# Cross-attention in split fp32: one PSUM bank for each unit of both products, first passes scaled in place, the bias and the residual waiting in the result tile

## The chip, the cores and the metric

The kernel runs on one NeuronCore of a Trainium2 chip. The metric is the device time of one execution in microseconds. A profile records one execution: its span runs from the first to the last instruction, and the device time is a little longer than the span. Five engines run side by side, each in the order of its own instruction list: PE (matrix products), DVE (vector), ACT (scalar), POOL and SP. SP and POOL mostly start DMA transfers; POOL also reduces across partitions. PE writes its sums into PSUM, a memory of eight banks of 128 x 512 fp32 values.

## What is computed

Eight batches, each with `x1` and `x2` of 512 channels by 1024 positions:

```python
q = jnp.einsum('bcn,dc->bnd', x1, Wq) + bq          # D = 64
k = jnp.einsum('bcn,dc->bdn', x2, Wk) + bk[:, None]
v = jnp.einsum('bcn,dc->bdn', x2, Wv) + bv[:, None] # 512 channels
attn = jax.nn.softmax(jnp.einsum('bnd,bdm->bnm', q, k), axis=2)
attn_out = jnp.einsum('bcm,bnm->bcn', v, attn)
return attn_out + x1
```

All of it is fp32. The two large products are "the value product" (v) and "the result product" (attn_out).

## The kernel before

**Splitting.** A plain fp32 product of 128 x 128 by 128 x 512 takes two records on PE, 0.43 us each on the chain that ended last (22 of them in 9.44 us); the type fp32r (fp32 rounded to fewer bits) takes one of 0.23 us (16 in 3.63 us). So an operand is split into a high part h, a low part l and a third part d = a mixture of the two scaled by T = 4096, and one exact product becomes three fp32r passes: h by h, l by l, d by d. h by h and l by l are summed in one PSUM bank ("X"), d by d in another ("Y"); the product is (T+1) times X joined with Y, up to a factor T.

**Units.** A batch has eight value units j (128 positions by 512 channels) and eight result units u (128 queries by 512 channels). A value unit takes 12 passes (`VX`: 8 into X, `VY`: 4 into Y); a result unit takes 24 (`R.u.m` for m = 0 to 7: one d pass into Y, then h and l into X). Before a value unit's `VY`, ACT writes the bias times T into the Y bank (`sy`). After it ACT copies Y to SBUF (`cy`), DVE joins X with it (`jn`), and the pair of units is split again: `vh` on ACT, `vl` and `vd` on DVE, 128 x 1024 values each. After a result unit ACT takes Y out, scaled by the reciprocal of the softmax sum (`oy`), DVE joins X with it (`o`), POOL adds x1 transposed by an accumulating DMA into the result tile (`oa`), and SP stores it (`st`). Units 6 and 7 of the first seven batches leave before the reciprocal is there, and ACT scales them later (`os`). The last batch's units 6 and 7 get x1 from a loaded tile on DVE (`lt`, `t`), and its unit 7 leaves in two parts (`o`, `p`).

**Scores and softmax.** `Q` and `K` are plain fp32 products (`qe`, `qd`, `qr`, `ql` and the same for k take them out, repeat and split them). `S.h.i` are the 16 blocks of scores of a batch, two passes each; `Sc` copies one to SBUF on ACT; `F` folds the maximum on DVE, `T` reduces it across partitions on POOL, `L` subtracts it on DVE, `E` takes the exponential on ACT, `H`, `l`, `d` split a unit of it. `es`, `a1` (an accumulating DMA from POOL), `a2`, `a3`, `tot` and `few` form the softmax sums of a quarter (two units), `rec` the reciprocal, `r2` two scaled copies of it.

**Batch one** (the first) has plain fp32 in three value units (`VF`, joined by `jf`) and in result units 0 and 1 (`RF`, taken out by `of`), since the split parts are not there yet.

**Order.** The order of all this is written out by hand as three strings of such words: FIRST for batch one, MIDDLE for the six that follow, LAST for the eighth. A word with "+" belongs to the next batch, with "-" to the one before. Each engine gets its own words in that order and the tile pools place the waits. PSUM: three X banks, three Y banks, two score banks ("sc"), each used in turn, so the fourth X unit waits until the first one's X bank has been read.

Of the kernel before, what the change touches and what calls it, by code (L numbers as in the profile page):

```python
# [35 lines left out]
vd.2 +Q +qe +ldx2.1 S.1.2 Sc.1.2 VY.6 cy.6 jn.6 S.1.3 Sc.1.3 S.1.4 Sc.1.4 S.1.5 Sc.1.5 T.1 L.3 S.1.6 Sc.1.6
VX.7 S.1.7 sy.7 VY.7 E.0 RF.0.0 RF.0.1 RF.0.2 RF.0.3 RF.0.4 RF.0.5 E.1 es.0 RF.1.0 a1.0 L.2 Sc.1.7 F.2 T.2
RF.1.1 E.3 H.3 l.3 a2.0 RF.1.2 RF.1.3 E.2 H.2 es.1 l.2 a1.1 a3.0 +qd +qr +ql RF.1.4 cy.7 jn.7 vh.3 +ldx2.0 +K
+ke RF.1.5 L.5 E.5 RF.0.6 L.4 E.4 H.4 RF.1.6 d.2 RF.0.7 RF.1.7 R.2.0 vl.3 tot.0 few.0 rec.0 r2.0 of.1 oa.1 F.3
of.0 d.3 es.2 R.2.1 R.2.2 R.2.3 R.2.4 R.2.5 R.3.0 R.3.1 R.3.2 R.3.3 R.3.4 a2.1 a3.1 +kc +kr +kl +S.0.0 +S.0.2  # L40
+Sc.0.0 H.5 l.4 R.3.5 st.1 +S.0.1 +Sc.0.1 +Sc.0.2 vd.3 R.2.6 R.3.6 T.3 L.6 L.7 E.7 +S.0.3 +Sc.0.3 R.2.7 R.3.7
d.4 R.4.0 R.4.1 a1.2 a2.2 +S.0.4 +S.0.5 tot.1 few.1 rec.1 oa.0 st.0 a3.2 l.5 d.5 E.6 H.6 l.6 d.6 tot.2 few.2
r2.1 oy.2 oy.3 o.2 o.3 oa.2 oa.3 st.2 st.3 H.7 l.7 rec.2 +Sc.0.4 +Sc.0.5 R.4.2 R.4.3 R.4.4 R.4.5 R.4.6 R.4.7
+S.0.6 +Sc.0.6 d.7 +S.0.7 +Sc.0.7 +F.0 es.3 a1.3 r2.2 oy.4 o.4 oa.4 st.4 +xh.0 +xl.0 +xd.0 +xh.1 +xl.1 R.5.0
R.5.1 R.5.2 R.5.3 R.5.4 R.5.5 R.5.6 R.5.7 oy.5 o.5 +T.0 +L.0 +L.1 +E.0 +E.1 +es.0 oa.5 st.5 a2.3 a3.3 +F.1
+xd.1 R.6.0 R.6.1 R.6.2 R.6.3 R.6.4 R.6.5 R.6.6 R.6.7 oy.6 o.6 +S.1.0 +xh.2 +xl.2 +xd.2 +sy.0 R.7.0 R.7.1
R.7.2 R.7.3 +xh.3 +xl.3 tot.3 few.3 rec.3 +sy.1 +Sc.1.0 +S.1.1 +Sc.1.1 R.7.4 R.7.5 R.7.6 R.7.7 oy.7 o.7
"""
MIDDLE = """
VY.0 cy.0 VX.0 +ldx1.0 a1.0 sy.2 jn.0 T.1 L.2 L.3 sy.3 VX.1 VY.1 cy.1 jn.1 H.1 l.1 H.0 l.0 d.0 vh.0 vl.0 vd.0  # L50
S.1.2 Sc.1.2 VY.2 cy.2 VX.2 jn.2 S.1.4 +ldx1.1 d.1 VY.3 cy.3 VX.3 jn.3 sy.4 E.2 S.1.3 Sc.1.3 Sc.1.4 sy.5 VX.4
-r2.3 -os.6 -oa.6 -st.6 S.1.5 Sc.1.5 xd.3 a2.0 a3.0 VY.5 cy.5 VX.5 vh.1 vl.1 vd.1 S.1.6 Sc.1.6 VY.4 cy.4 jn.4
# [24 lines left out]
r2.2 oy.4 oy.5 o.4 oa.4 st.4 l.7 o.5 oa.5 st.5 d.7 R.7.0 R.7.7 rec.3 r2.3 oy.6 oy.7 t.6 t.7 o.6 o.7 p.7 st.6
st.7 sq.7
# [4 lines left out]
def kernel(  # L83
# [31 lines left out]
    seed = const.tile([P, C], F32, name="bv_seed")  # L115
# [18 lines left out]
    class Batch:  # L134
        def __init__(self, b):
            self.b = b
            self.first = b == 0
            self.final = b == B - 1
            self.x1, self.x2, self.ps = {}, {}, {}
            self.half, self.fold, self.top, self.es, self.den, self.few, self.r = {}, {}, {}, {}, {}, {}, {}  # L140
            self.c, self.e, self.v, self.v4 = {}, {}, {}, {}
            self.X, self.Y, self.y, self.o = {}, {}, {}, {}
# [65 lines left out]
        def take_out(self, which):  # L210
            t = new([P, N], "es" if self.first else "v4", f"{'qk'[which]}_{self.b}")
            for h, r in ((0, lo), (1, hi)):
                nc.scalar.activation(
                    t[r, ts(h, H)], self.ps[which][r, :], AF.Identity, bias=bqk_sb[r, which : which + 1]
                )
            return t
# [43 lines left out]
        def S(self, h, i):  # L260
            self.ps[h, i] = ps = bank("Y" if self.first and i % 2 else "sc", f"ps_s_{self.b}_{h}_{i}")
# [42 lines left out]
        def d(self, u):  # L304
            e = self.e[u]
            e["d"] = new([P, MT, P], "kd", f"ed_{self.b}_{u}", FR)
            nc.vector.scalar_tensor_tensor(e["d"], f32(e["l"]), -T, f32(e["h"]), ALU.mult, ALU.add)  # L307
# [29 lines left out]
        def rec(self, Q):  # L337
            self.r[Q] = new([P, 2, 2], "r", f"r_{self.b}_{Q}")
            nc.vector.reciprocal(self.r[Q][:, 0, :], self.few[Q])

        def r2(self, Q):
            r = self.r[Q]
            nc.scalar.mul(r[:, 1, :], r[:, 0, :], 1.0 / T)
            nc.scalar.mul(r[:, 0, :], r[:, 0, :], 1.0 + 1.0 / T)
# [26 lines left out]

        def VF(self, j, c):
            if c == 0:
                self.X[j] = bank("X", f"ps_v_{self.b}_{j}")
            nc.tensor.matmul(  # L375
                self.X[j], self.chunk(j // 2)[:, c, ts(j % 2, P)], wraw[c // 2][:, c % 2, :],
# [3 lines left out]
        def pair(self, j):  # L380
            if j % 2 == 0:
                tag = ("kh" if j < 4 else "kl") if self.first else "v4"
                self.v4[j // 2] = new([P, 2, C], tag, f"v4_{self.b}_{j // 2}")
            return self.v4[j // 2][:, j % 2, :]

        def jf(self, j):
            nc.vector.scalar_tensor_tensor(self.pair(j), self.X[j], T, seed, ALU.mult, ALU.add)

        def sy(self, j):
# [196 lines left out]
```

## Time and profile before

| what | value |
|---|---|
| time, median of 3 runs | 660.4 us (660.15 to 660.41) |
| span of the profiled execution | 657.9 us |
| the profiled execution's own device time | not given apart from the runs; the median lies 2.5 us over the span |
| PE busy | 652.4 us (99%), 2797 products |
| DVE busy | 615.3 us (94%) |
| ACT busy | 451.0 us (69%) |
| POOL busy | 204.6 us (31%) |
| DMA | 90.21 MB, 137 GB/s over the span |

Busy times are sums over instructions of one engine. PE's records overlap: one lasts 0.39 us and the next starts 0.23 us after it. So the pace of PE is read from the chain that ended last, where each piece counts only the step.

### The profile page before, as it was taken

The numbers are of one execution on the slowest core, as the hardware profiler recorded it, in microseconds if no ns is written. First come the engines' busy times: TensorE is split into PE (matmuls) and PEld (weight loads), VectorE is DVE, ScalarE is ACT, GpSimd is POOL, SyncE is SP. The second block draws the span as 40 slices with busy tenths as digits, with TensorE's granted clock in tenths as the row PEclk, the third lists the DMA queues.
The fourth block names the chain that finished last, engine by engine and source line by source line (L and its number), as shares of the span: only waits on it lengthen the run. The fifth ranks groups of instructions, "written<-read, shape, count | busy, mean of one in ns | idle before, by whom it ended". The sixth has DMA issues, their size and how long they took to land.

```text
span 657.9 us, 8049 instructions
## 1 busy us (share of the span) xinstructions
PE 652.4 (99%) x2797; PEld 491.6 (75%) x2797; DVE 615.3 (94%) x689; ACT 451.0 (69%) x668; POOL 204.6 (31%) x162
## 2 busy tenths in 40 slices
PE   9999999999999999999999999999999999999997
PEld 3664888668886688866888668886688776887786
DVE  5789999999999999999999999999999999989994
ACT  5597748767587675875767767687675975759541
POOL 0024532423314343033520335221352214412451
PEclk9999999999999999999999999999999999999999
DMA  8544466564656556374563746737467274642374
GB/s 312 197 143 85 96 134 185 102 187 90 143 152 148 140 115 167 104 200 108 117 173 90 210 96 121 170 83 220 81 128 185 73 206 100 124 113 48 64 137 136
DMA packets 41464, 90.21 MB, mean 137 GB/s; under 512 B 13136, under 2 KB 13904, under 8 KB 37712
## 3 DMA queue, kind: packets, MB, share of 16 engines
q0 software_dynamic: 13536, 33.04, 30.1%
q1 hardware_dynamic: 27168, 56.14, 25.7%
q10 hardware_dynamic: 720, 0.53, 0.2%
q8 instruction: 22, 0.36, 0.2%
q14 instruction: 18, 0.15, 0.1%
HBM read 51.91 MB, written 16.78 MB: 104 GB/s over the span
## 4 chain that ended last, share of the span: by engine, by line
PE 94%; DVE 3%; ACT 2%; issue 0%; DVEq 0%; ACTq 0%
PE ps_oX L435 33%; PE ps_oY L435 17%; PE ps_vX L395 15%; PE ps_s L263 8%; PE ps_vY L395 8%; PE ps_k L206 4%; PE ps_q L206 4%; PE ps_o L460 2%; PE ps_v L375 2%; PE ps_warm L535 1%; DVE vd L427 1%; DVE vl L422 0%; DVE v L413 0%; ACT ps_vY L391 0%; DVE ed L307 0%; DVE e L291 0%
## 5 line engine op out<-in xcount | busy, mean ns | idle before, releaser
L435 PE MATMUL ps_oY<-vd,ed 128*128 128x512 f32 x496 | 193.8, 393 | 0.2 <-DVE ed L307 0.2
L435 PE MATMUL ps_oX<-vh,eh 128*128 128x512 f32 x496 | 193.0, 389 | 0.0
L435 PE MATMUL ps_oX<-vl,el 128*128 128x512 f32 x496 | 193.0, 389 | 0.0
L435 PEld LDWEIGHTS ps_oY<-vd,ed 128*128 128x128 f32 x496 | 93.1, 188 | 25.1 <-issue 5.3
L515 POOL DMA_DIRECT2D o<-in_x1T_dram x62 | 55.6, 917 | 172.2 <-ACT o L512 100.0
L435 PEld LDWEIGHTS ps_oX<-vl,el 128*128 128x128 f32 x496 | 93.0, 188 | 20.2
L435 PEld LDWEIGHTS ps_oX<-vh,eh 128*128 128x128 f32 x496 | 93.1, 188 | 19.5 <-DVE v L413 0.3
L294 ACT ACTIVATE e<-e 128x1024 f32<-128x1024 f32 x64 | 67.7, 1061 | 54.7 <-DVE e L291 53.6
L268 ACT COPY e<-ps_s 128x512 f32<-128x512 f32 x128 | 71.0, 591 | 32.7 <-PE ps_s L263 31.8
L330 POOL PARTITION_ALL_REDUCE den<-es x32 | 82.1, 2565 | 23.3 <-DVE es L320 20.2
L316 POOL DMA_DIRECT2D es<-e x32 | 28.6, 894 | 181.7 <-ACT es L313 172.3
L307 DVE SCALAR_TENSOR_TENSOR ed<-el,eh 128x1024 fp32r<-128x1024 f32 x62 | 81.9, 1321 | 2.1
L302 DVE TENSOR_TENSOR el<-e,eh 128x1024 fp32r<-128x1024 f32 x62 | 79.7, 1302 | 0.0
L291 DVE TENSOR_TENSOR e<-e,top 128x1024 f32<-128x1024 f32 x64 | 76.1, 1220 | 1.0 <-POOL top L283 1.0
L283 POOL PARTITION_ALL_REDUCE top<-max x32 | 46.8, 1463 | 65.3 <-DVE max L279 65.2
L395 PE MATMUL ps_vX<-wh,xh 128*128 128x512 f32 x244 | 66.1, 393 | 0.0
L395 PE MATMUL ps_vX<-wl,xl 128*128 128x512 f32 x244 | 65.2, 389 | 0.0
L395 PE MATMUL ps_vY<-wd,xd 128*128 128x512 f32 x244 | 64.7, 392 | 0.4 <-ACT ps_vY L391 0.4
L298 ACT ACTIVATE eh<-e 128x1024 fp32r<-128x1024 f32 x62 | 64.7, 1055 | 0.5
L410 ACT COPY vy<-ps_vY 128x512 f32<-128x512 f32 x61 | 36.0, 592 | 37.5 <-PE ps_vY L395 37.3
L395 PEld LDWEIGHTS ps_vX<-wh,xh 128*128 128x128 f32 x244 | 45.3, 188 | 14.3 <-DVE max L278 4.1
L395 PEld LDWEIGHTS ps_vY<-wd,xd 128*128 128x128 f32 x244 | 45.5, 188 | 11.8 <-issue 1.3
(59 smaller groups left out, 963.3 us busy)
## 6 DMA issues: line engine op xcount, KB each, us to landing
x<-in_x_dram SPq DMA_DIRECT2D x29, 1024.0 KB, 7.0
es<-e POOLq DMA_DIRECT2D x32, 512.0 KB, 4.9
out_dram<-o SPq DMA_DIRECT2D x63, 256.0 KB, 2.4
o<-in_x1T_dram POOLq DMA_DIRECT2D x62, 256.0 KB, 4.2
x<-in_x_dram SPq DMA_DIRECT2D x5, 512.0 KB, 10.4
k<-k SPq DMA_DIRECT2D x16, 128.0 KB, 2.3
q<-q SPq DMA_DIRECT2D x16, 128.0 KB, 2.4
w_raw<-in_wvT_dram SPq DMA_DIRECT2D x4, 256.0 KB, 3.7
```

What stands on the lines that cost most here:

```text
L206: nc.tensor.matmul(ps[r, :], wqk_sb[:, which, c, :], x(h, c), start=(c == 0), stop=(c == CT - 1))
L263: nc.tensor.matmul(ps, k[:, ts(i, P)], self.qa[:, ts(h, H)], start=(z == 0), stop=(z == 1))
L268: nc.scalar.copy(self.half[h][:, :, i, :], self.ps[h, i].rearrange("p (q n) -> p q n", q=2))
L291: nc.vector.tensor_tensor(e, e, top, ALU.subtract)
L294: nc.scalar.activation(self.unit(u), self.unit(u), AF.Exp)
L298: nc.scalar.activation(self.e[u]["h"], self.unit(u), AF.Copy, scale=SPLIT)
L302: nc.vector.tensor_tensor(self.e[u]["l"], self.unit(u), f32(self.e[u]["h"]), ALU.subtract)
L307: nc.vector.scalar_tensor_tensor(e["d"], f32(e["l"]), -T, f32(e["h"]), ALU.mult, ALU.add)
L330: nc.gpsimd.partition_all_reduce(self.den[Q], self.es[Q][:, 0, :], P, ReduceOp.add)
L395: nc.tensor.matmul(ps, self.c[j // 2][z][:, c, ts(j % 2, P)], w[z][:, c, :], start=(start and c == 0), stop=(stop and c == CT - 1), skip_g ...
L435: nc.tensor.matmul(ps, self.e[u][z][:, m, :], self.v[m // 2][z][:, m % 2, :], start=start, stop=stop, skip_group_check=True,)
L515: nc.gpsimd.dma_start(self.o[u], x1T[self.b, ts(u, P), :], accum_op=ALU.add)
```

## The change

1. **One bank for a unit.** X and Y pools go; a unit of either product has one bank out of five ("B"), and the scores get three. The h and l passes (`VX`, or `R` which is now two passes) are summed, ACT scales the bank in place (`vf` by -(T+1), `fx` by 1 + 1/T), and the d passes (`VY`, or `D.u.m`, one pass each) are added on top. The d part of the exponentials is scaled by -1/T to suit.
2. **Values are split straight out of PSUM**: `vh` on ACT and `vl` on DVE read the bank, one unit (512) at a time. `sy`, `cy`, `jn`, `jf` go.
3. **The result leaves in one step.** The value bias is no longer in v. SP fills the result tile with the bias (`lo`, 256 KB each), POOL adds x1 to it by DMA (`oa`), and DVE's `ev` multiplies the bank by the reciprocal and adds the tile. `oy`, `os`, `r2`, `of`, `t`, `p`, `lt` go. The result tiles are four instead of three. In the last batch unit 7 leaves in two parts (`ew`, `ev`) ahead of unit 6.
4. **Batch one** has two plain fp32 value units instead of three and no plain result units.
5. **All three strings are written anew**; of them only the first line stands here.

```diff
 FIRST = """
-wh.0 VF.0.0 VF.1.0 wl.0 VF.0.1 VF.1.1 wd.0 w4.0 wh.1 VF.0.2 VF.1.2 wl.1 VF.0.3 wd.1 w4.1 ldx2.0 lwq VF.2.0
+wh.0 VF.1.0 wl.0 ldx2.0 wd.0 ldx2.1 wh.1 VF.0.0 VF.1.1 VF.0.1 VF.0.2 wl.1 VF.1.2 xh.1 w4.0 w4.1 xh.2 VF.0.3 xl.1
...
-    BUFS = {"X": 3, "Y": 3, "sc": 2, "raw": 2, "top": 2, "kh": 5, "kl": 5, "kd": 4, "es": 2, "few": 2, "r": 2, "y": 2, "o": 3, "x": 2}
-    WHOLE = 3
-    LATE = (6, 7)
+    BUFS = {"B": 5, "sc": 3, "raw": 2, "top": 2, "kh": 5, "kl": 5, "kd": 4, "es": 2, "few": 2, "r": 2, "o": 4, "x": 2}
+    WHOLE = 2
...
-            self.ps[h, i] = ps = bank("Y" if self.first and i % 2 else "sc", f"ps_s_{self.b}_{h}_{i}")
+            self.ps[h, i] = ps = bank("B" if self.first and i % 2 else "sc", f"ps_s_{self.b}_{h}_{i}")
...
-            nc.vector.scalar_tensor_tensor(e["d"], f32(e["l"]), -T, f32(e["h"]), ALU.mult, ALU.add)
+            nc.vector.scalar_tensor_tensor(e["d"], f32(e["h"]), -1.0 / T, f32(e["l"]), ALU.mult, ALU.add)
...
+        def VX(self, j):
+            self.B[j] = bank("B", f"ps_v_{self.b}_{j}")
+            self.vpass(j, "h", True, False)
+            self.vpass(j, "l", False, True)
+
+        def vf(self, j):
+            nc.scalar.activation(self.B[j], self.B[j], AF.Copy, scale=T if self.whole(j) else -(T + 1.0))
+
         def VY(self, j):
+            self.vpass(j, "d", False, True)
...
+        def vh(self, j):
+            nc.scalar.activation(self.vpart(j, "h"), self.B[j], AF.Copy, scale=SPLIT / T)
+
+        def vl(self, j):
+            h = f32(self.v[j // 2, "h"])[:, j % 2, :]
+            nc.vector.scalar_tensor_tensor(self.vpart(j, "l"), h, -T, self.B[j], ALU.mult, ALU.add)
...
         def R(self, u, m):
             if m == 0:
+                self.B[u] = bank("B", f"ps_o_{self.b}_{u}")
+            self.rpass(u, m, "h", m == 0, False)
+            self.rpass(u, m, "l", False, m == MT - 1)
+
+        def fx(self, u):
+            nc.scalar.activation(self.B[u], self.B[u], AF.Copy, scale=1.0 + 1.0 / T)
+
+        def D(self, u, m):
+            self.rpass(u, m, "d", False, m == MT - 1)
+
+        def lo(self, u):
             self.o[u] = new([P, C], "o", f"o_{self.b}_{u}")
+            nc.sync.dma_start(self.o[u], bv.broadcast_to([P, C]))
...
+        def leave(self, u, at):
+            o = self.o[u][:, at]
+            nc.vector.scalar_tensor_tensor(o, self.B[u][:, at], self.share(u), o, ALU.mult, ALU.add)
```

What the new strings do to the engines shows at three places. The first is PE in batch one, where result units 0 and 1 begin. In these rows `e` holds the exponentials, `v4` the joined values of two units, and `eh`, `el`, `vh`, `vl` the split parts. Before:

```order
L460 MATMUL ps_o_0_406<-v4_0_0_145,e_0_275 128x512 x2
L460 MATMUL ps_o_0_406<-v4_0_1_147,e_0_275 128x512 x2
L460 MATMUL ps_o_0_406<-v4_0_2_228,e_0_275 128x512 x2
L460 MATMUL ps_o_1_416<-v4_0_0_145,e_0_275 128x512 x2
L460 MATMUL ps_o_1_416<-v4_0_1_147,e_0_275 128x512 x2
```

and now:

```order
L418 MATMUL ps_o_0_397<-vh_0_129,eh_0_367 128x512
L418 MATMUL ps_o_0_397<-vl_0_172,el_0_376 128x512
L418 MATMUL ps_o_0_397<-vh_1_240,eh_0_367 128x512
L418 MATMUL ps_o_0_397<-vl_1_244,el_0_376 128x512
L418 MATMUL ps_o_0_397<-vh_2_254,eh_0_367 128x512
L418 MATMUL ps_o_0_397<-vl_2_279,el_0_376 128x512
```

Units 0 and 1 now take the split parts of the exponentials and of the values; their d passes follow later in the row.

The second place is PE at the start of a middle batch (the third one), where value units begin. Before:

```order
L395 MATMUL ps_vY_0_1487<-wd,xd_0_1390 128x512 x4
L395 MATMUL ps_vX_0_1574<-wh,xh_0_1386 128x512 x4
L395 MATMUL ps_vX_0_1574<-wl,xl_0_1388 128x512 x4
L395 MATMUL ps_vX_1_1596<-wh,xh_0_1386 128x512 x4
L395 MATMUL ps_vX_1_1596<-wl,xl_0_1388 128x512 x4
L395 MATMUL ps_vY_1_1566<-wd,xd_0_1390 128x512 x4
L263 MATMUL ps_s_1_2_1628<-qa_1220,kh_1309 128x512
L263 MATMUL ps_s_1_2_1628<-qa_1220,kl_1311 128x512
```

and now:

```order
L379 MATMUL ps_v_1_1424<-wd,xd_0_1433 128x512 x4
L262 MATMUL ps_s_1_4_1570<-qa_1178,kh_1294 128x512
L262 MATMUL ps_s_1_4_1570<-qa_1178,kl_1311 128x512
L379 MATMUL ps_v_3_1577<-wh,xh_1_1456 128x512 x4
L379 MATMUL ps_v_3_1577<-wl,xl_1_1538 128x512 x4
L262 MATMUL ps_s_1_1_1596<-qa_1178,kh_1294 128x512
L262 MATMUL ps_s_1_1_1596<-qa_1178,kl_1311 128x512
L379 MATMUL ps_v_5_1605<-wh,xh_2_1493 128x512 x4
L379 MATMUL ps_v_5_1605<-wl,xl_2_1495 128x512 x4
L379 MATMUL ps_v_2_1615<-wh,xh_1_1456 128x512 x4
L379 MATMUL ps_v_2_1615<-wl,xl_1_1538 128x512 x4
```

Value units 0 and 1 have moved their X passes into the batch before, and unit 2 takes the bank that unit 1 leaves: between unit 1's last pass and unit 2's first stand two score blocks and the X passes of units 3 and 5.

The third place is SP's queue around the end of batch one's stores. Before:

```order
L150 DMA x_2_0_872<-in_x_dram 128x2048
L150 DMA x_2_1_941<-in_x_dram 128x2048
L519 DMA out_dram<-o_6_795 128x512
L335 DMA few_0_1029<-den_0_1027 128x1x1 x2
L519 DMA out_dram<-o_7_855 128x512
```

and now:

```order
L437 DMA o_5_808<-in_bv_dram 128x512
L437 DMA o_7_826<-in_bv_dram 128x512
L457 DMA out_dram<-o_4_687 128x512
L157 DMA x_2_0_910<-in_x_dram 128x2048
L457 DMA out_dram<-o_7_826 128x512
L157 DMA x_2_1_984<-in_x_dram 128x2048
L457 DMA out_dram<-o_6_803 128x512
L437 DMA o_1_1022<-in_bv_dram 128x512
L457 DMA out_dram<-o_5_808 128x512
L437 DMA o_0_1053<-in_bv_dram 128x512
```

The fills of the result tiles with the bias stand among the stores and loads, and each waits in line for the store of the tile that it reuses.

More of the change, by code (lines that the diff above doesn't have):

```diff
@@ L36 @@
[L36 to L40, printed above, removed]
@@ L210, in take_out @@
         def take_out(self, which):
-            t = new([P, N], "es" if self.first else "v4", f"{'qk'[which]}_{self.b}")
+            t = new([P, N], "es" if self.first else "qk", f"{'qk'[which]}_{self.b}")
             for h, r in ((0, lo), (1, hi)):
@@ L337, in rec @@
         def rec(self, Q):
[L338 to L344, printed above, removed]
+            self.r[Q] = new([P, 2], "r", f"r_{self.b}_{Q}")
+            nc.vector.reciprocal(self.r[Q], self.few[Q])
         def chunk(self, k):
@@ L370, in xd, with whole @@
             )
+        def whole(self, j):
+            return self.first and j < WHOLE
         def VF(self, j, c):
             if c == 0:
-                self.X[j] = bank("X", f"ps_v_{self.b}_{j}")
+                self.B[j] = bank("B", f"ps_v_{self.b}_{j}")
             nc.tensor.matmul(
-                self.X[j], self.chunk(j // 2)[:, c, ts(j % 2, P)], wraw[c // 2][:, c % 2, :],
+                self.B[j], self.chunk(j // 2)[:, c, ts(j % 2, P)], wraw[c // 2][:, c % 2, :],
                 start=(c == 0), stop=(c == CT - 1),
@@ L378, in VF @@
             )
[L380 to L389, printed above, removed]
-            self.Y[j] = bank("Y", f"ps_vY_{self.b}_{j}")
-            nc.scalar.copy(self.Y[j], seed)
@@ L403, in VX @@
-        def VX(self, j):
-            self.X[j] = bank("X", f"ps_vX_{self.b}_{j}")
-            self.vpass(j, "h", self.X[j], True, False)
-            self.vpass(j, "l", self.X[j], False, True)
-        def cy(self, j):
-            self.y[j] = new([P, C], "y", f"vy_{self.b}_{j}")
-            nc.scalar.copy(self.y[j], self.Y[j])
-        def jn(self, j):
-            nc.vector.scalar_tensor_tensor(self.pair(j), self.X[j], -(T + 1.0), self.y[j], ALU.mult, ALU.add)
-        def vh(self, p):
-            self.v[p] = {"h": new([P, 2, C], f"vh{p}", f"vh_{self.b}_{p}", FR)}
-            nc.scalar.activation(self.v[p]["h"], self.v4[p], AF.Copy, scale=SPLIT / T)
@@ L419, in vl @@
-        def vl(self, p):
-            v = self.v[p]
-            v["l"] = new([P, 2, C], f"vl{p}", f"vl_{self.b}_{p}", FR)
-            nc.vector.scalar_tensor_tensor(v["l"], f32(v["h"]), -T, self.v4[p], ALU.mult, ALU.add)
+        def VX(self, j):
+            self.B[j] = bank("B", f"ps_v_{self.b}_{j}")
+            self.vpass(j, "h", True, False)
+            self.vpass(j, "l", False, True)
+        def vf(self, j):
+            nc.scalar.activation(self.B[j], self.B[j], AF.Copy, scale=T if self.whole(j) else -(T + 1.0))
@@ L424, in vd, with rpass @@
         def vd(self, p):
-            v = self.v[p]
-            v["d"] = new([P, 2, C], f"vd{p}", f"vd_{self.b}_{p}", FR)
-            nc.vector.tensor_tensor(v["d"], f32(v["h"]), f32(v["l"]), ALU.subtract)
+            v = new([P, 2, C], f"vd{p}", f"vd_{self.b}_{p}", FR)
+            nc.vector.tensor_tensor(v, f32(self.v[p, "h"]), f32(self.v[p, "l"]), ALU.subtract)
+            self.v[p, "d"] = v
         def ends(self, u):
             return self.final and u == MT - 1
-        def rpass(self, u, m, z, ps, start, stop):
+        def rpass(self, u, m, z, start, stop):
@@ L440, in R @@
         def R(self, u, m):
-            top = MT - 1
             if m == 0:
-                self.X[u] = bank("X", f"ps_oX_{self.b}_{u}")
-                self.Y[u] = bank("Y", f"ps_oY_{self.b}_{u}")
-            if self.ends(u) and m == 0:
-                for i in range(MT):
-                    self.rpass(u, i, "d", self.Y[u], i == 0, i == top)
-            elif self.ends(u) and m == top:
-                for i in range(MT):
-                    self.rpass(u, i, "h", self.X[u], i == 0, False)
-                    self.rpass(u, i, "l", self.X[u], False, i == top)
-            elif not self.ends(u):
-                self.rpass(u, m, "d", self.Y[u], m == 0, m == top)
-                self.rpass(u, m, "h", self.X[u], m == 0, False)
-                self.rpass(u, m, "l", self.X[u], False, m == top)
@@ L457, in RF @@
-        def RF(self, u, m):
-            if m == 0:
-                self.X[u] = bank("X", f"ps_o_{self.b}_{u}")
-            nc.tensor.matmul(
-                self.X[u], self.unit(u)[:, m, :], self.v4[m // 2][:, m % 2, :],
-                start=(m == 0), stop=(m == MT - 1),
-            )
-        def share(self, u, k):
-            return self.r[u // 2][:, k, u % 2 : u % 2 + 1]
-        def fresh(self, u):
-            self.o[u] = new([P, C], "o", f"o_{self.b}_{u}")
-            return self.o[u]
@@ L472, in of @@
-        def of(self, u):
-            nc.scalar.activation(self.fresh(u), self.X[u], AF.Copy, scale=self.share(u, 1))
-        def late(self, u):
-            return u in LATE and not self.final
-        def given(self, u):
-            return self.final and u >= MT - 2
-        def oy(self, u):
-            self.y[u] = new([P, C], "y", f"oy_{self.b}_{u}")
-            if self.late(u):
-                nc.scalar.copy(self.y[u], self.Y[u])
-            else:
-                nc.scalar.activation(self.y[u], self.Y[u], AF.Identity, scale=self.share(u, 1))
@@ L488, in lt @@
-        def lt(self):
-            t = new([P, CT, H], "x", "x1T_last")
-            self.x1t = {MT - 2 + i: t[:, i, :] for i in range(2)}
-            src = x1T[self.b].rearrange("(u p) c -> p u c", p=P)[:, MT - 2 :, :]
-            nc.sync.dma_start(t[:, 0:2, :], src)
-        def t(self, u):
-            nc.vector.tensor_tensor(self.y[u], self.x1t[u], self.y[u], ALU.subtract)
-        def leave(self, u, o, at):
-            scale = T + 1.0 if self.late(u) else self.share(u, 0)
-            sign = ALU.add if self.given(u) else ALU.subtract
-            nc.vector.scalar_tensor_tensor(
-                o[:, at], self.X[u][:, at], scale, self.y[u][:, at], ALU.mult, sign
-            )
@@ L504, in o_ @@
-        def o_(self, u):
-            self.leave(u, self.fresh(u), left if self.ends(u) else slice(0, C))
-        def p(self, u):
-            self.o[u, 1] = new([P, C], "o", f"o_{self.b}_{u}_right")
-            self.leave(u, self.o[u, 1], right)
-        def os(self, u):
-            nc.scalar.mul(self.o[u], self.o[u], self.share(u, 1))
+                self.B[u] = bank("B", f"ps_o_{self.b}_{u}")
+            self.rpass(u, m, "h", m == 0, False)
+            self.rpass(u, m, "l", False, m == MT - 1)
@@ L517, in st, with ev, ew @@
+        def leave(self, u, at):
+            o = self.o[u][:, at]
+            nc.vector.scalar_tensor_tensor(o, self.B[u][:, at], self.share(u), o, ALU.mult, ALU.add)
+        def ev(self, u):
+            self.leave(u, left if self.ends(u) else slice(0, C))
+        def ew(self, u):
+            self.leave(u, right)
         def st(self, u):
@@ L532, in begin @@
         for i, times in enumerate((3, 3, 3)):
-            ps = bank("Y", f"ps_warm{i}")
+            ps = bank("B", f"ps_warm{i}")
             for k in range(times):
```

119 lines of the change are left out of this document (67 added, 52 removed).

## The prediction

> **What bounds the kernel now.** I read the busy times, then PE's waits, then the chain that ended last, then PE's rows where a stage begins.
>
> ```profile
> span 657.9 us, 8049 instructions
> PE 652.4 (99%) x2797; PEld 491.6 (75%) x2797; DVE 615.3 (94%) x689; ACT 451.0 (69%) x668; POOL 204.6 (31%) x162
> PEclk9999999999999999999999999999999999999999
> ```
>
> ```profile
> PE ps_vY L395 <- ACT ps_vY L391: 0.4, 1, 0.4
> PE ps_s L263 <- ACT e L268: 0.2, 1, 0.2
> PE ps_oY L435 <- DVE ed L307: 0.2, 1, 0.2
> ```
>
> ```profile
> 4.86 9.44 PE ps_v L375 x22
> 47.45 9.44 PE ps_o L460 x22
> 56.89 3.58 PE ps_k L206 x16
> 103.15 3.63 PE ps_vX L395 x16
> 183.73 3.63 PE ps_vX L395 x16
> 650.60 3.65 PE ps_oX L435 x16
> ```
>
> ```profile
> 102.08 1.07 PE L395 MATMUL ps_vY<-wd,xd 128*128 128x512 f32 x4
> ...
> 583.92 1.07 PE L395 MATMUL ps_vY<-wd,xd 128*128 128x512 f32 x4
> ```
>
> PE is the bound: busy all the time at full clock, with 0.8 us of named waits. The chain gives its paces: an fp32r pass 3.63/16 = 0.227 us, a plain fp32 record 9.44/22 = 0.429 us (two per product, 0.858 us), a `Q` or `K` 3.58 us. Three stages, counted with these paces:
>
> - FIRST, 4.86 to 102.08 us = 97.2 us. Work: 56 fp32 records 24.0, four `Q`/`K` 14.3, 256 passes 58.1: 96.4 us. Nothing idle beyond some restarts.
> - MIDDLE, (583.92 - 102.08)/6 = 80.3 us each. Work: 96 + 32 + 192 = 320 passes 72.6, `Q` and `K` 7.2: 79.8 us. PE alone sets it.
> - LAST, 583.92 to 650.60 + 3.65 = 654.25 us: 70.3 us. Work: 300 passes, 68.1 us. Here 2.2 us are lost, the only place with a reserve.
>
> So a change pays only by taking work from PE, by those 2.2 us, or in the tail after 654.25; lighter DVE and ACT are worth nothing by themselves, but a new wait of PE costs in full.
>
> **The change, part by part.**
>
> *Batch one.* Sixteen `RF` products and four of `VF` go, 20 x 0.858 = 17.2 us; 60 passes come, 13.6 us. **-3.5 us on PE.** The other PE work stays: 96 value, 32 score and 192 result passes per later batch.
>
> *Vector and scalar work.*
>
> ```profile
> L413 DVE SCALAR_TENSOR_TENSOR v<-ps_vX,vy 128x512 f32<-128x512 f32 x61 | 41.0, 684 | 5.9 <-ACT vy L410 4.6 <-PE ps_vX L395 1.3
> L422 DVE SCALAR_TENSOR_TENSOR vl<-vh,v 128x1024 fp32r<-128x1024 f32 x32 | 40.2, 1258 | 1.8 <-ACT vh L417 1.4
> L500 DVE SCALAR_TENSOR_TENSOR o<-ps_oX,r,oy 128x512 f32<-128x512 f32 x47 | 34.3, 745 | 3.3 <-ACT oy L486 3.3
> L302 DVE TENSOR_TENSOR el<-e,eh 128x1024 fp32r<-128x1024 f32 x62 | 79.7, 1302 | 0.0
> L368 DVE SCALAR_TENSOR_TENSOR xd<-xl,xh 128x1024 fp32r<-128x1024 f32 x30 | 41.7, 1392 | 0.7
> L391 ACT COPY ps_vY<-bv_seed 128x512 f32<-128x512 f32 x61 | 35.9, 603 | 0.1
> L410 ACT COPY vy<-ps_vY 128x512 f32<-128x512 f32 x61 | 36.0, 592 | 37.5 <-PE ps_vY L395 37.3
> L417 ACT ACTIVATE vh<-v 128x1024 fp32r<-128x1024 f32 x32 | 33.9, 1059 | 13.3 <-DVE v L413 11.8 <-DVE v L387 1.5
> L486 ACT ACTIVATE oy<-ps_oY,r 128x512 f32<-128x512 f32 x48 | 31.1, 681 | 13.3 <-PE ps_oY L435 13.1
> L294 ACT ACTIVATE e<-e 128x1024 f32<-128x1024 f32 x64 | 67.7, 1061 | 54.7 <-DVE e L291 53.6
> ```
>
> ```profile
> 102.40:182.67 80.27, 80.27 (x353) 61.59 (x352) 78.81 (x89) 56.94 (x87) 26.56 (x21) 1.00 0.60 144
> ```
>
> In this middle batch DVE is busy 78.8 of 80.3 us. Eight `jn` go (8 x 0.684 = 5.5); `vl` becomes eight of 512 out of PSUM, at `jn`'s price, for four of 1.258 (+0.4); `ev` costs what `o` did (0.745). DVE falls to about 73.8 us. ACT loses eight each of `sy`, `cy`, `oy` and four `vh` (4.8 + 4.7 + 5.4 + 4.2 = 19.1) and gets 24 of 512 (`vf`, `vh`, `fx`). Scaling a bank in place is not in the trace: SBUF to PSUM took 0.603, PSUM to SBUF 0.592, with a scale from memory 0.681; I take 0.60, for the scale here is a constant. ACT falls by 4.7 us. Both gains lie under PE: worth nothing, except as slack.
>
> *New waits of PE.* Two are added. The d passes wait for ACT's scaling of that bank, and a unit's first pass waits until the bank of five units ago is read out. I summed the work between the ends of such waits:
>
> - Middle batch, bank for value unit 2: freed by unit 1's `vl`. On DVE stand, from the previous batch's last pass on, `ev.7` 0.745, `xd.1` 1.392, `l.0` 1.302, `vl.1` 0.684: 4.1 us. PE has 4 + 20 passes, 5.4 us. Slack 1.3.
> - Result unit 7's bank, freed by `ev.2`: DVE has `d.5` (as `l`, 1.3), `xd.0` 1.392, `a3.3` (under 0.7), `ev.2` 0.745, 4.1 us; PE 22 passes, 5.0 us. Slack 0.9.
> - `fx.1` ahead of `D.1.0`: ACT has `E.5`, `es.2` (about 1.06 each), `fx.3`, `fx.1`: 3.3 us even if it only starts when `R.1.7` ends; PE 19 passes, 4.3 us. Slack 1.0. In batch one only four passes, 0.9 us, stand between `R.1.7` and `D.1.0`, for 0.6 of `fx.1`: 0.3.
> - Score bank, `S.0.3` to `S.0.1`: four passes, 0.9 us, against one `Sc` of about 0.6. Slack 0.3.
>
> All positive, some thin. Behind a waiting `vl` or `ev` on DVE queue the next units' parts, so a late one returns as the next bank's wait. Middle batches: between 0 and 0.4 us each (a thin slack overrun by one 0.68 operation); I take 0.05, **+0.3 in all**, since every slack summed is positive.
>
> *Batch one's start.* Fills and loads move: `ldx2.1` goes ahead of `lwq` on SP, the bias load behind the x1 loads.
>
> ```profile
> 13.27 2.00 ACT L358 ACTIVATE xh<-x 128x1024 fp32r<-128x1024 f32 x2 [0.78 <-DMA x<-in_x_dram]
> ...
> 23.50 1.39 ACT L213 ACTIVATE q<-ps_q,bqk_sb 64x512 f32<-64x512 f32 x2 [1.01 <-PE ps_q L206]
> ...
> 27.71 1.06 ACT L236 ACTIVATE qa<-q 128x1024 fp32r<-128x1024 f32 x1 [1.11 <-DMA q<-q]
> ```
>
> `VF` ends at 4.86 + 6.86 = 11.7, the X passes of units 2 and 3 at 15.4, `K` at 19.0, `Q` at 22.7, against 23.4 before. The second half of x2 had landed by 13.27 (the wait in that row), ahead of `K`; x1 had by 23.4 - 3.6 = 19.8 at the latest, and if it lands no sooner `Q` waits 0.8. ACT needs 27.71 + 1.06 - 23.50 = 5.3 us from `Q`'s end to the rounded q, DVE some 1.3 more: 29.3. PE meanwhile has 32 passes, 7.3 us, to 30.0. It fits with 0.7 to spare. The weights' l part (two ACT operations of 1.06 behind `xh.1`) and `R.0` and `R.2`, whose l parts come just in time, are as thin. I add **+0.6 us**, between 0 and 3 (one late `l`, 1.3 us, at two places).
>
> *Last batch.* The three named waits (0.8 us) sit on `sy`, `Sc` and `d`:
>
> ```profile
> 598.11 1.19 PE L395 MATMUL ps_vY<-wd,xd 128*128 128x512 f32 x4 [0.43 <-ACT ps_vY L391]
> ```
>
> `sy` goes and DVE is lighter. Of the new waits there I summed two. `S.1.7` needs `Sc.1.0`: after value unit 0's X passes ACT has `vf.0` 0.6, five operations of 1.06 (two `E`, `es`, two `H`) and two `Sc`, 7.1 us; PE has 40 passes, 9.1. `R.6.0` needs `ev.0` after `D.0.7`: 0.745 and a short reciprocal against nine passes, 2.0 us. Both hold. Of the 2.2 us I count about half back: **-1.2**, between 0 and -2.2.
>
> *Tail.*
>
> ```profile
> 654.28 0.48 DVE L500 SCALAR_TENSOR_TENSOR o<-ps_oX,r,oy 128x256 f32<-128x256 f32 x1 [1.57 <-PE ps_oX L435]
> 654.68 0.47 DVE L500 SCALAR_TENSOR_TENSOR o_right<-ps_oX,r,oy 128x256 f32<-128x256 f32 x1
> ```
>
> ```profile
> out_dram<-o SPq DMA_DIRECT2D x63, 256.0 KB, 2.4
> o<-in_x1T_dram POOLq DMA_DIRECT2D x62, 256.0 KB, 4.2
> bv_seed<-in_bv_dram SPq DMA_DIRECT2D x1, 256.0 KB, 8.8
> out_dram<-o_right SPq DMA_DIRECT2D x1, 128.0 KB, 1.8
> ```
>
> Now one `ev.6` of 0.745 stands for two halves (0.9), but a store of 256 KB (2.4) for one of 128 KB (1.8): **+0.45**, between 0.2 and 0.9.
>
> Sum: -3.5 + 0.3 + 0.6 - 1.2 + 0.45 = **-3.4**: span 654.5, and with the 2.5 us that the median has over this span, **657.0 us**. With every bound low: -3.5 - 2.2 + 0.2 = 654.9; with every bound high: -3.5 + 2.4 + 3 + 0.9 = 663.2.
>
> **Rivals.**
>
> *The saving is spent on new waits.* One bank per unit makes a unit hold its bank through the scaling and both kinds of passes. If an operand is 0.5 us later than summed in each middle batch, 6 x 0.55 = 3.3 us go: no change, 660. For it speaks that five slacks are at or below 1.0 us and DVE is still at 92% (73.8 of 80.3); against it that the old order, at 98% DVE, left PE no wait in these batches. The Trainium skill, Perfetto Trace Analysis, Optimization Strategy, says of a gap that repeats on the engine that should be saturated that there may be too little SBUF or PSUM for the next tile; by that rule the five-bank ring would show such a gap. The trace of before has none in its middle batches, and cannot show the new ring.
>
> *The fills hold up the results: slower.* Each `lo` waits in SP's line for the store of the tile it reuses, POOL's `oa` waits for it, `ev` for that, and DVE's line stands behind.
>
> ```profile
> L515 POOL DMA_DIRECT2D o<-in_x1T_dram x62 | 55.6, 917 | 172.2 <-ACT o L512 100.0 <-DVE o L500 62.1 <-ACT o L473 6.9
> ```
>
> ```profile
> 655.21 0.38 SPq L522 DMA_DIRECT2D out_dram<-o_right  x1
> ```
>
> From `D.2.7` to `D.7.7`, PE has 78 passes, 17.7 us. `ev.2` takes 4.1 of it (above), its store 2.4 to land, three issues on SP 0.38 each: the last `lo` starts 10.1 us before `ev.7` is due. A fill landing like a store (2.4) and `oa` (0.9 to issue, 4.2 to land) take 7.5: in time. At 8.8, as the one bias load in the trace, they take 13.9: 3.8 late, less the slack of 1.3 for value unit 2's bank, 2.5 us a batch, 15 in all, 672 us. It takes back the forecast's 3.4 us (0.57 a batch) from a landing of 6.9 us on. Against it: that bias load stood behind the loads of w, x2 and wqk, 3.3 MB by their sizes, and the 64 fills add 16.8 MB to DMA engines at a share of 0.60 (the middle batch's row).
>
> **How the numbers follow.** A measurement of this kernel tells 0.2%, 1.3 us: 659.1 and 661.7 are the limits. Forecast, PE's saved work arrives: 0.72, with 654.9 to 659.1. New waits eat it up: 0.18, of which 0.12 within the limits and 0.06 above. Fills: 0.10, all above. The range 654.8 to 662.0 leaves out the fills and the worst of the waits.
>
> **What would show it.** PE 2817 products, its chain without L460's pieces, a middle batch still at 80.3 us, no PE wait on a scaled bank, DVE near 584 us (615.3 - 61 x 0.684 for `jn`, + 64 x 0.684 - 40.2 for `vl`, + 1.5 for two more `ev`, + 5.2 for the `l` and `d` of two more units). Wrong if value or result passes wait for `ev` or `vl` in every middle batch, or if `oa` ends DVE's idle time.

## The result, and the profile after

The changed kernel takes **664.45 us** (median of 4 runs, 663.9 to 667.68) against 660.27 (659.94 to 660.41): ratio 1.0075, 95% interval 1.0053 to 1.0097. It is 4.2 us slower; 3.4 us faster was forecast. The profiled execution took 663.9 us for a span of 662.1.

The head of its page, and PE's row of the 40 slices:

```profile
span 662.1 us, 8012 instructions
PE 651.1 (98%) x2817; PEld 496.6 (75%) x2817; DVE 573.0 (87%) x661; ACT 401.7 (61%) x565; POOL 207.2 (31%) x164
PE   9999999999999999999999999999999999999967
```

The products are those forecast (2817), and PE shows less than 90% in the last two slices only. PE's waits, and its rows at the longest of them (start, us, engine, line, tiles; in brackets the idle time before):

```profile
PE ps_o L418 <- DVE o L447: 5.6, 1, 5.6
PE ps_warm L473 <- DVE spark L468: 1.0, 1, 1.0
PE ps_o L418 <- DVE vd L409: 0.2, 1, 0.2
...
627.66 1.53 PE L418 MATMUL ps_o<-vd,ed 128*128 128x512 f32 x6
634.80 0.76 PE L418 MATMUL ps_o<-vh,eh 128*128 128x512 f32 x1 [5.61 <-DVE o L447]
```

One wait of 5.61 us stands out (the 1.0 us is the start of the program, in both kernels). The row at 634.80 is `R.6.0` of the last batch, which needs the bank that `ev.0` reads out. DVE's rows show why `ev.0` is late:

```profile
611.52 1.21 DVE L306 SCALAR_TENSOR_TENSOR ed<-eh,el 128x1024 fp32r<-128x1024 f32 x1
...
615.53 0.41 DVE L319 TENSOR_TENSOR es<-es 128x256 f32<-128x256 f32 x1
615.87 1.21 DVE L306 SCALAR_TENSOR_TENSOR ed<-eh,el 128x1024 fp32r<-128x1024 f32 x1
617.00 1.21 DVE L409 TENSOR_TENSOR vd<-vh,vl 128x1024 fp32r<-128x1024 f32 x1
...
623.81 1.21 DVE L301 TENSOR_TENSOR el<-e,eh 128x1024 fp32r<-128x1024 f32 x1
632.40 0.17 DVE L338 RECIPROCAL r<-few 128x2 f32<-128x2 f32 x1 [7.38 <-DMA few<-den]
632.50 1.23 DVE L301 TENSOR_TENSOR el<-e,eh 128x1024 fp32r<-128x1024 f32 x1
633.65 0.16 DVE L338 RECIPROCAL r<-few 128x2 f32<-128x2 f32 x1
633.91 1.41 DVE L447 SCALAR_TENSOR_TENSOR o<-ps_o,r,o 128x512 f32<-128x512 f32 x2
```

DVE works without a gap until 625.02 and then stands for 7.38 us at `rec.1`, the reciprocal for quarter 1. `rec.0` and `ev.0`, which need quarter 0 alone, are queued behind it. `rec.1` waits for `few.1`, which SP issued only at 626.71 (and which landed just before 632.40), because POOL's sum over partitions (`tot.1`) had just ended:

```profile
606.80 2.69 POOL L329 PARTITION_ALL_REDUCE den<-es  x1 [4.84 <-DVE es L319]
...
610.66 3.61 POOL L440 DMA_DIRECT2D o<-in_x1T_dram  x4
616.11 10.58 POOL L329 PARTITION_ALL_REDUCE den<-es  x1 [1.83 <-issue]
...
636.47 1.79 POOL L329 PARTITION_ALL_REDUCE den<-es  x1 [7.24 <-DVE es L319]
```

`tot.1` lasted 10.58 us; the other 31 sums of this kernel took 1.79 to 2.70, and the 32 of the kernel before 1.79 to 2.85. No row of the kernel before shows a sum that long.

By stages (columns as in the prediction: window, us, then PE, PEld, DVE, ACT, POOL busy, granted clock, DMA share, GB/s), first the kernel before, then the changed one:

```profile
4.70:102.08 97.38, 97.38 (x378) 62.60 (x376) 85.19 (x95) 68.58 (x97) 27.97 (x21) 1.00 0.58 159
583.92:654.25 70.33, 69.48 (x301) 55.57 (x299) 60.11 (x73) 40.33 (x64) 21.76 (x18) 1.00 0.46 94
```

```profile
4.79:104.81 100.02, 99.82 (x420) 70.57 (x420) 85.92 (x98) 68.81 (x97) 29.61 (x22) 1.00 0.65 185
104.81:185.20 80.39, 80.39 (x353) 61.94 (x352) 73.45 (x85) 51.80 (x73) 25.85 (x22) 1.00 0.66 165
587.28:657.91 70.63, 65.00 (x279) 52.90 (x277) 52.89 (x65) 30.00 (x44) 28.67 (x17) 0.98 0.54 118
```

The new strings put 22 more passes of each next batch (20 of its values, two of its scores, 5.0 us) into the stage ahead of it, so FIRST grows and LAST should shrink. LAST does not: its 278 passes (the window counts one more, which began before it) are 63.1 us of work, and it takes 70.6.

### The profile page after: what moved, and what is told of

It reads as the page before. It is cut to its first block, busy times and chain, and to the rows that moved or that the text cites. A ratio compares the mean times of both kernels' runs of the same rounds, so it can differ in the third digit from the quotient of the medians.

```text
span 662.1 us, 8012 instructions
## 1 busy us (share of the span) xinstructions
PE 651.1 (98%) x2817; PEld 496.6 (75%) x2817; DVE 573.0 (87%) x661; ACT 401.7 (61%) x565; POOL 207.2 (31%) x164
## 5 line engine op out<-in xcount | busy, mean ns | idle before, releaser
L418 PE MATMUL ps_o<-vh,eh 128*128 128x512 f32 x512 | 200.9, 392 | 5.6 <-DVE o L447 5.6
L418 PE MATMUL ps_o<-vl,el 128*128 128x512 f32 x512 | 200.0, 391 | 0.0
L418 PE MATMUL ps_o<-vd,ed 128*128 128x512 f32 x512 | 141.0, 393 | 0.2 <-DVE vd L409 0.2
L418 PEld LDWEIGHTS ps_o<-vh,eh 128*128 128x128 f32 x512 | 96.3, 188 | 31.8 <-issue 11.7
L418 PEld LDWEIGHTS ps_o<-vd,ed 128*128 128x128 f32 x512 | 96.5, 189 | 21.8 <-DVE vd L409 0.6
L418 PEld LDWEIGHTS ps_o<-vl,el 128*128 128x128 f32 x512 | 96.4, 188 | 20.4 <-DVE el L301 0.2
L306 DVE SCALAR_TENSOR_TENSOR ed<-eh,el 128x1024 fp32r<-128x1024 f32 x64 | 83.1, 1306 | 1.1 <-PE ps_o L418 1.1
L379 PE MATMUL ps_v<-wh,xh 128*128 128x512 f32 x248 | 66.9, 391 | 0.0
L379 PE MATMUL ps_v<-wl,xl 128*128 128x512 f32 x248 | 66.3, 389 | 0.0
L379 PE MATMUL ps_v<-wd,xd 128*128 128x512 f32 x248 | 65.4, 392 | 0.0
```

What stands on the lines that cost most here:

```text
L306: nc.vector.scalar_tensor_tensor(e["d"], f32(e["h"]), -1.0 / T, f32(e["l"]), ALU.mult, ALU.add)
L379: nc.tensor.matmul(self.B[j], self.c[j // 2][z][:, c, ts(j % 2, P)], w[z][:, c, :], start=(start and c == 0), stop=(stop and c == CT - 1), ...
L418: nc.tensor.matmul(self.B[u], self.e[u][z][:, m, :], self.v[m // 2, z][:, m % 2, :], start=start, stop=stop, skip_group_check=True,)
```

## The experiments

Two questions were open: is the wait what the chain above says, and what makes one sum over partitions last 10.58 us? For the second there were two theories. **Shut-out:** from 610.4 to 625.02 us all fourteen operations that DVE runs read two SBUF operands (`L`, `d`, `a2`, `a3`, `vd`, `l`), one behind the other; POOL's sum, which reads SBUF too, gets in only when this run ends, and it ended 1.67 us after it. **DMA queue:** POOL had just started four accumulating transfers in a row (610.66), and the sum waits for them.

Each kernel is the changed one with the edit shown. Its time stands against runs of the kernel before on the same chip (660.7 us in the first four, 660.6 in the next four).

### `rec.1` behind `ev.0`

```diff
-... D.2.1 rec.1 D.3.3 E.6 es.3 D.0.4 D.3.4 H.6 l.6 ... rec.0 D.2.2 D.3.6 H.7 ev.0 D.3.7 ...
+... D.2.1 D.3.3 E.6 es.3 D.0.4 D.3.4 H.6 l.6 ... rec.0 D.2.2 D.3.6 H.7 ev.0 rec.1 D.3.7 ...
```

> In the last batch the reciprocal of quarter 1 (rec.1) is put behind ev.0 in DVE's order; it stood five DVE operations ahead of it. Chain theory: R.6.0's wait of 5.61 us comes from DVE standing at rec.1, whose sums are late; ev.0 needs only quarter 0, which had long landed. Then DVE goes on with l.6 as soon as ACT has H.6 (27.67 + 1.06 = 628.7 us in the changed kernel's timeline), ev.0 ends near 631.1, and 1.9 us of the wait is left; ev.3 (behind rec.1) ends near 633.5 and R.4.0, 18 passes after R.6.0, finds its bank free. Time 664.4 - 3.7 = 660.7 us. Rival, the result tile: if ev.0 is held by its own tile (the bias fill and the added x1 came late) the wait stays at 5 to 6 us and the time at 664.4.

660.27 us, ratio 0.9995 (0.9982 to 1.0008). On DVE two operations (`l.6` and `rec.0`) stood between `rec.1` and `ev.0`, which makes three places, not five. The wait shrank as expected; `tot.1` still took 10.58 us:

```profile
PE ps_o L418 <- DVE o L447: 1.9, 1, 1.9
```

So some 4 us (664.45 - 660.27) are the place of one 0.17 us operation in DVE's order. The result tile held nothing up.

### A break in DVE's run

```diff
+    gap = const.tile([P, H], F32, name="gap")
+        def pause(self, Q):
+            nc.vector.memset(gap, 0.0)
-... oa.1 d.2 a3.1 H.5 d.0 R.1.4 vd.1 ...
+... oa.1 d.2 a3.1 H.5 d.0 pause.1 R.1.4 vd.1 ...
```

> One DVE operation that reads nothing from SBUF (a memset of a spare 128x512 tile, read by nobody) is put behind d.0 in the last batch, in the middle of DVE's unbroken run from 610.4 to 625.0 us. Shut-out theory: the 10.58 us of POOL's sum over partitions (tot.1) are a wait for DVE, whose eight operations in a row all read two SBUF operands; the break lets POOL in. Then tot.1 takes 2 to 4 us, few.1 lands near 625, rec.1 holds nobody, R.6.0 waits at most 0.5 us, and the time is about 659 us, 5 less. DVE is longer by the memset and by what it waits for POOL, some 1 to 2 us, which the last batch's later operations can bear. DMA-queue theory: the 10.58 us come from the four accumulating transfers that POOL started just before; then tot.1 stays at 10 to 11 us, the wait at 5.6, and the time at 664.4 to 665.

657.69 us, ratio 0.9959 (0.9946 to 0.9971). POOL's row and DVE's:

```profile
615.56 2.63 POOL L333 PARTITION_ALL_REDUCE den<-es  x1 [1.83 <-issue]
```

```profile
616.59 0.48 DVE L329 MEMSET gap<- 128x512 f32 x1
617.00 1.57 DVE L413 TENSOR_TENSOR vd<-vh,vl 128x1024 fp32r<-128x1024 f32 x1
```

An operation that does nothing, added to an engine, makes the changed kernel 6.8 us faster. The sum takes 2.63 us, the `vd` behind the memset 1.57 instead of 1.21 (now DVE waits for POOL), and PE's wait for `ev.0` is gone.

### A larger memory for POOL's transfers

```diff
-    ... num_devices=1, dynamic_dma_scratch_size=4096)
+    ... num_devices=1, dynamic_dma_scratch_size=8192)
```

> The memory set aside for the transfers that POOL writes out itself is doubled, from 4096 to 8192 bytes; nothing else. DMA-queue theory: four accumulating transfers in a row overfill it and the reduction behind them waits until it empties; then tot.1 falls from 10.58 us to 2 to 5, the wait at R.6.0 to 0 to 1, the time to 659 to 660. Shut-out theory: nothing changes, tot.1 10 to 11 us, wait 5.6, 664.4 us.

665.27 us, ratio 1.0071 (1.0059 to 1.0083); `tot.1` 10.58 us, wait 5.6. The DMA-queue theory falls in this form.

### No fill and no added x1

```diff
-            nc.sync.dma_start(self.o[u], bv.broadcast_to([P, C]))
+            nc.sync.dma_start(self.o[u], x1T[self.b, ts(u, P), :])
...
-            nc.gpsimd.dma_start(self.o[u], x1T[self.b, ts(u, P), :], accum_op=ALU.add)
+            return
```

> The value bias is left out of the result: SP loads x1 transposed straight into the result tile, and POOL's accumulating transfers of x1 (oa) go, all 64. Shut-out theory: DVE's run in the last batch stands as it is, so tot.1 still takes about 10 us, R.6.0 still waits 5 to 6 us, and the time is 664 us within 0.7. DMA-queue theory: with no transfer ahead of it tot.1 takes at most 2.7 us, the wait is gone, 659 us. Fills theory (the rival of the prediction: fills and added x1 hold up ev and so the next units): a middle batch falls from 80.4 us by what they cost; since PE shows no named wait there I expect 80.3 to 80.4, so at most 0.7 us over the seven batches.

664.49 us, ratio 1.005 (1.0037 to 1.0063). The sum, with no transfer ahead of it, and a middle batch:

```profile
617.30 10.58 POOL L329 PARTITION_ALL_REDUCE den<-es  x1 [5.31 <-DVE es L319]
```

```profile
106.17:186.56 80.39, 80.39 (x354) 61.96 (x352) 73.41 (x84) 51.82 (x73) 20.40 (x13) 1.00 0.49 138
```

This kernel leaves the value bias out; each result tile still gets one transfer, a load of x1 where the fill stood. The DMA-queue theory falls altogether. So does the price of the prediction's second rival (2.5 us a batch): with one transfer for each tile in place of two, a middle batch takes the same 80.39 us.

### What kind of operation shuts POOL out

Four more kernels put another operation at the memset's place behind `d.0`. First one with two SBUF operands:

```diff
+        def again(self, p):
+            nc.vector.tensor_tensor(gap, f32(self.v[p, "h"]), f32(self.v[p, "l"]), ALU.subtract)
```

> At the same place behind d.0, in place of the memset, one more DVE operation that does read two SBUF operands: the difference of pair 1 (vd.1) a second time, 128x1024, into a spare tile that nobody reads. Shut-out theory: such an operation lets nobody in and makes the unbroken run one step (1.13 us) longer; tot.1 takes 10.58 + 1.13 = 11.7 us, R.6.0 waits 5.6 + 1.1 = 6.7 us, time 664.4 + 1.1 = 665.5 us. Rival, the shift: any additional operation there changes the meeting of the two engines; then tot.1 takes 2 to 4 us and the time is about 658 as with the memset.

667.88 us, ratio 1.0103 (1.0088 to 1.0119). The sum grew by the operation's 1.14 us step, and the wait to 6.7:

```profile
618.84 11.72 POOL L333 PARTITION_ALL_REDUCE den<-es  x1 [1.83 <-issue]
```

The time is 2.4 us over what was expected; about 2 of them lie elsewhere in the profiled execution (batch one took 1.3 us longer there, and the second batch has a wait of 0.8 us for an `ev`).

Then a copy, with one SBUF operand:

```diff
+        def pause(self, Q):
+            nc.vector.tensor_copy(gap, f32(self.v[1, "h"])[:, 0, :])
```

> At the same place behind d.0 a DVE operation with one SBUF operand instead of none or two: a plain copy of 128x512 fp32 from vh into a spare tile that nobody reads. If what shuts POOL out is the second operand, the copy lets POOL in as the memsets did: tot.1 2.6 us, R.6.0 waits at most 0.1 us, 657 to 659 us. If any reading operation of that size shuts it out, the run is longer by the copy: tot.1 10.6 us plus the copy's time (0.3 to 0.6, by the memset's 0.48), R.6.0 waits about 6 us, about 665 us. The Trainium skill, SBUF — State Buffer, Who interferes with whom, says that a copy between SBUF tiles can enter a mode in which DVE takes both ports and shuts GpSimd out; by that it is the second case.

666.35 us, one run beside one of the kernel before at 659.97. The sum and the copy:

```profile
617.33 10.91 POOL L333 PARTITION_ALL_REDUCE den<-es  x1 [1.83 <-issue]
```

```profile
618.22 0.42 DVE L329 COPY gap<-vh 128x512 f32<-128x512 f32 x1
```

10.91 is 10.58 and the copy's step of 0.34. So, by this one run, one SBUF operand is enough here, if the operation is a copy; the second operand alone is not what matters.

Then the shortest break:

```diff
+        def pause(self, Q):
+            nc.vector.memset(spark, 0.0)
```

> At the same place the shortest break: a memset of 128x1, nothing read from SBUF, against the 128x512 that took 0.48 us. Theory 'one free moment is enough': POOL is only waiting for a moment in which DVE reads no two SBUF operands; tot.1 takes about 2.6 us, R.6.0 doesn't wait, time 657.7 us. Rival 'the break must last': POOL needs a stretch of several tenths of a us; then tot.1 stays at 10.6 us, the wait at 5.6, the time at 664.4.

658.27 us, ratio 0.9964 (0.9947 to 0.998).

```profile
618.17 2.63 POOL L332 PARTITION_ALL_REDUCE den<-es  x1 [1.83 <-issue]
```

```profile
619.08 2.10 DVE L412 TENSOR_TENSOR vd<-vh,vl 128x1024 fp32r<-128x1024 f32 x1
619.09 0.06 DVE L328 MEMSET spark<- 128x1 f32 x1
```

0.06 us are enough. POOL then has its turn, and DVE's next operation takes 2.10 us for 1.21.

Last, the same break without an operation more: `rec.0`, which DVE has to do anyway, in that place.

```diff
-... a2.1 lo.2 R.3.5 ... d.0 R.1.4 vd.1 ... oa.0 few.0 R.2.7 ...
+... a2.1 lo.2 few.0 R.3.5 ... d.0 rec.0 R.1.4 vd.1 ... oa.0 R.2.7 ...
-... D.2.1 rec.1 D.3.3 ... D.3.5 rec.0 D.2.2 ... ev.0 D.3.7 ...
+... D.2.1 D.3.3 ... D.3.5 D.2.2 ... ev.0 rec.1 D.3.7 ...
```

> No operation added: rec.0 (0.16 us, reads one SBUF operand of 128x2) is put behind d.0, with few.0 put up on SP so that it can; rec.1 behind ev.0. If one free moment is enough, tot.1 takes about 2.6 us, R.6.0 doesn't wait, time 657.5 us (the memset's 657.7 without the memset). If the break must last, tot.1 stays at 10.6 us, and with rec.1 out of the way a wait of about 1.8 us is left as in the run with rec.1 alone moved: 660.2 us.

**657.05 us**, ratio 0.9952 (0.9939 to 0.9966): faster than both kernels, with nothing in it but three words moved. `rec.0` reads one SBUF operand, of 128x2, and lets POOL in as the memsets did. `tot.1` 2.63 us; the last stage has no wait left (PE's last pass ends at 651.06, just behind this window):

```profile
587.60:650.90 63.30, 63.30 (x279) 52.00 (x277) 53.77 (x65) 30.00 (x44) 20.72 (x17) 1.00 0.61 131
```

### Two more edits on top of it

```diff
-... fx.2 d.3 D.0.0 ... R.4.2 vd.3 L.6 ...
+... fx.2 vd.3 d.3 D.0.0 ... R.4.2 L.6 ...
-D.6.2 D.6.3 ew.7 sw.7 ev.7 st.7 D.6.4 D.6.5 D.6.6 D.6.7 ev.6 st.6
+D.6.2 D.6.3 ev.7 st.7 D.6.4 D.6.5 D.6.6 D.6.7 ew.6 sw.6 ev.6 st.6
-            return self.final and u == MT - 1
+            return self.final and u == MT - 2
```

> The version before with two more edits: in batch one vd.3 ahead of d.3 on DVE (D.0.6 lost 0.32 to 0.36 us there), and in the last batch unit 6, which is the last to leave, in two parts instead of unit 7. The end after PE's last product was 3.65 us in the kernel before and 4.2 in the changed one; I expect 3.7, so 0.5 + 0.3 = 0.8 us less than the version before: 656.7 us if tot.1 is short, 659.4 if it stays at 10.6. Rival: the end is set by the landing of a store whatever its size, and only 0.3 us come.

657.32 us, ratio 0.9954 (0.9942 to 0.9966): no better than the version before. `D.0.6`'s wait went, and 0.5 us for an `el` and 0.3 for ACT's `es` came in batch one. From PE's last pass to the end it took 4.1 us (656.5 - 652.4) against 4.2 there (655.3 - 651.1): unit 6 leaving in two parts is worth 0.1 us, not 0.5, as the rival had it.

## Why the prediction was wrong, point by point

| term | forecast | changed kernel | with `rec.0` up, `rec.1` back |
|---|---|---|---|
| PE work of batch one | -3.5 | -3.5 | -3.5 |
| losses in batch one | +0.6 | +1.2 | +1.6 |
| middle batches | +0.3 | +0.6 | +0.8 |
| last batch | -1.2 | +5.3 | -1.9 |
| tail | +0.45 | +0.55 | +0.6 |

Each column but the first is read from the windows: a stage's length less its work at the prediction's paces (FIRST now 97.9 us, LAST 63.1), against the same for the kernel before (1.0 and 2.3 us lost). The sums are 4.15 and -2.4; the spans differ by 4.2 and -2.6. The rest lies in the start (FIRST begins at 4.79 and 4.54 us for 4.70) and in rounding.

- **The step that failed** is the last batch: "Of the new waits there I summed two ... `R.6.0` needs `ev.0` after `D.0.7`: 0.745 and a short reciprocal against nine passes, 2.0 us." The two operations were counted, and not what stood ahead of them in DVE's line: `rec.1`, which hangs on `tot.1` and `few.1`, a chain of POOL, SP and a DMA landing. Asking what is queued ahead of `ev.0` would have shown it. In place of the 1.2 us that were to come back, the last batch lost 5.3 more than before; this one wait is 5.6. With `rec.1` alone moved, 4.2 us came back.
- **The length of `tot.1`** was not asked for either. At 2.6 us for 10.58 even the order as it stood lost nothing (the kernels with a memset). The new order put fourteen operations on SBUF in one row without a pause; the sum began during the seventh and stood behind it and the seven after it; no other sum took over 2.70 us. The row that could have warned was the spread of the sums in the kernel before, 1.79 to 2.85 us for one form. The loss needed both things: taking away the one gave back 4.2 us, the other 6.8, both 7.4.
- **PE's saved work** was right: the three versions in which POOL got in by a memset or by the order of the reciprocals alone stand at 657.05 to 658.27, and the forecast, which had no such wait, stood at 657.0. That it agrees so closely is partly luck: with `rec.0` up the last batch gave back 1.9 us instead of 1.2, batch one lost 1.0 more than counted (PE's row falls some 0.5 us behind its pace at each of three places: `VX.2` waiting for `xh`, then for `xl`, and `D.0.6` for `vd`), and 2.5 us were added between span and time where the profiled executions show 1.8.
- **In-place scaling** was right: `fx` 0.585 us, `vf` 0.593 for 0.60. PE waited on no scaled bank, and the middle batches cost 0.1 us each.
- **DVE** is at 573.0 us, not 584; `vd` fell from 1.43 to 1.22 us each, and `ql` from 1.81 to 1.22, which the prediction had left as they were. It had no bearing.
- **The rivals.** "The saving is spent on new waits" had the right kind, a unit's bank given back late, but in the wrong place: middle batches, 0.55 us each. They lost a tenth of a microsecond each; in three of the experiments' profiles one of the six waited 0.6 to 0.9 us at `R.5.0` for an `ev`. The fills landed in 4.6 us by the median, under the 6.9 from which they would have counted. DVE stood for an added x1 twice, 2.1 us in all, and PE waited for neither; the experiment without fill and addition agrees.
- **One sum** of the prediction is off without effect: its steps up to `Q`'s end in batch one (11.7 and three of 3.6) add up to 22.5 us, not 22.7. Both sides of the comparison that follows start there, so the slack of 0.7 stands.

## What to carry to other kernels

When a wait is summed, list the engine's whole line ahead of the operation that ends it, and follow each of those back to what it waits for. A long row of DVE operations on SBUF can hold up a POOL instruction for as long as the row lasts: put a tiny one such as a reciprocal into the row where POOL's result is due, as was tried here. An instruction that takes several times its usual length in one place is a wait that no list of waits names.

## What the runs showed of the hardware

**DVE and POOL.** In a row of DVE operations on SBUF that never paused, a sum over partitions did not get in for eight of them in succession; a DVE operation of 0.06 us without an SBUF operand let it in. The Trainium skill, SBUF — State Buffer, Who interferes with whom, says that a DVE instruction with two SBUF inputs contends with a GpSimd instruction that reads SBUF, that a copy in a two-port mode does too, and that the one issued second blocks until the first finishes. The traces agree on which kinds do it (sums of 11.72 us with two operands, 10.91 with a copy, 2.63 with a memset); whether the copy ran in such a mode no run shows. They differ on how long in this place: the sum stood behind the first operation and behind seven more.

That is no rule for every row. In a middle batch of the changed kernel a sum began during `ed`, and had its turn when that one ended, although `xl`, with two SBUF operands too, stood directly behind:

```profile
322.28 2.43 POOL L329 PARTITION_ALL_REDUCE den<-es  x1
...
321.83 1.22 DVE L306 SCALAR_TENSOR_TENSOR ed<-eh,el 128x1024 fp32r<-128x1024 f32 x1
322.96 2.12 DVE L357 TENSOR_TENSOR xl<-x,xh 128x1024 fp32r<-128x1024 f32 x1
```

This time DVE waited: `xl` took 2.12 us, against 1.22 for the `ed` ahead of it. Nor was DVE halted by ACT there: `xh`, which ACT makes for `xl`, had ended at 317.64. So a long row can shut POOL out and a break lets it in; what decides, without a break, which of the two engines waits is open.

**The clock after a wait.** The 5.6 us wait cost 1.4 us more than itself: the first eight passes from `R.6.0` on took 3.24 us, against 1.85 with `rec.0` up, where nothing waits. PE's granted clock (the column after POOL's) in the changed kernel, and with `rec.1` alone moved, where the wait was 1.9 us:

```profile
634.80:638.60 3.80, 3.80 (x11) 3.04 (x12) 1.54 (x3) 0.00 (x0) 1.79 (x1) 0.62 0.40 141
```

```profile
631.10:634.90 3.80, 3.73 (x16) 3.11 (x17) 2.21 (x5) 0.00 (x0) 0.17 (x1) 1.00 1.00 243
```

11 products in 3.8 us after the long wait, 16 after the short one; in the first 2 us after the long one the granted clock was 0.50. The Trainium skill, TensorE: Matmul & The Clock Gate, Part 1: The HAM clock gate, says that TensorE falls to half its clock after an idle window of about 3.4 us; both waits agree with that.
